# A graph layer's product held back for the last scatter, a table tile read in five parts, and its loads moved to another queue

## The chip, the cores and the metric

The kernel runs on one core of a Trainium2 chip. The core has five engines that this text names as the profile does: PE (TensorE, matrix products; PEld is its weight load), DVE (VectorE), ACT (ScalarE), POOL (GpSimd) and SP (SyncE, which here only issues transfers). [...] The metric is device microseconds of one launch, median of several runs.

## The reference

The input is a matrix x of 625 nodes by 1024 features and a list of 10,000 edges. Two layers follow each other. What matters here is layer 0:

```python
xn = layernorm(x)
x = x + gnn(xn, edges) + mix(xn)            # a graph attention, and a linear attention with an output product W_o
x = x + ffn(layernorm(x))                   # a product with weights rounded to -1, 0, 1
# gnn: for each edge e: s -> d and each of 4 heads
score[e, h] = sum_k leaky_relu(xl[s, h, k] + xr[d, h, k]) * att[h, k]
out[d, h]   = sum_e softmax_over_edges_into_d(score)[e, h] * xl[s, h]
# gnn ends with out @ W_up
```

Layer 1 has another graph step, another linear attention, and a feed-forward part with eight experts of which each node uses two; it takes the larger part of the time.

## The kernel before, in words

The 625 nodes are five tiles of 125 rows (`NT` = 5, `P` = 125). Nearly all products are in float32, with a moving side of 512 or 313 columns. In layer 0 the graph attention and the linear attention are computed side by side.

**Edge scores.** POOL gathers the rows xl and xr of each edge (`gather`, L621), 128 edges at a time and two such chunks to a group; DVE turns them into scores (`score_group`), ACT takes the exponential (L608), and POOL scatters the four numbers of each edge into a table in DRAM with a row per pair of nodes (`scatter`, L641). All scatters write one DRAM tensor, so each waits for the landing of the one before. Every node's edge to itself is written by ACT's queue (`self_loops`). CT, in SBUF, counts how often each pair of nodes occurs.

**Pacing.** The order of the instructions on each engine is written by hand. `do(prep, pe, after)` records a step: PE's part now, and its `after` part when the next step is recorded. `work(us)` adds to a planned time, and as it grows `one_beat` records one more group's gathers, scores and scatters between the products of the linear attention. What is left of the beats is recorded in the loop `while chunks: one_beat()`.

**Around the change.** `mixed(t)` (L758) is the output product of the linear attention for node tile t, in two halves c of 512 columns, each of 8 matmuls (`cs` selects halves); it leaves its sum open in PSUM, for `up_again` to add the graph attention to. The end of the edge stage records mixed(3), the rest of mixed(0), then mixed(1) and mixed(2) with `ternary`, the rounding of the feed-forward weights on DVE (L801, L802, L804) between them, and then the remaining beats. mixed(4) comes later, as the PSUM of tile 0 comes free.

After the last scatter, for each node tile p in turn:
- `load_table(p)` reads tile p of the table, `tb`, 125 partitions by five rows of 2000 bytes (500 numbers) each, 1.25 MB, through `rows_dma`, which splits every load into 112 and 13 partitions;
- `weigh(p)` multiplies it with CT on DVE, one instruction for each of the five source tiles s (L865), giving pT;
- `sums(p)` has 20 small matmuls of PE (pg: 4 heads by 5 source tiles), whose result DVE divides (dens, den, go; L898 to L902);
- `turn_sums(p)` transposes it, and `up_again(p)` adds its product with W_up to px and then, on DVE, px to x (L933);
- `ffn(p)` is the feed-forward part of tile p, in steps put between the others.

The rows of x are loaded again for this (L1056), and `add_bias` (L1072) adds the output bias to them. In the kernel before POOL issues all of this: table tile 0, x tile 0, table tile 1, then x tiles 1 to 4, and table tiles 2 to 4 as buffers of the pool `mid` come free. SP issues the weights (`Half`, L124), among them the key and value weights of layer 1 (`lin1.weights`).

[...]

Of the kernel before, what the change touches and what calls it, by code (L numbers as in the profile page):

```python
# [14 lines left out]
ALU = mybir.AluOpType  # L15
# [5 lines left out]
NT = 5  # L21
P = 125
# [31 lines left out]
def attempt(ctx: ExitStack, tc: tile.TileContext, w: dict, out: bass.AP, shifted: bool):  # L54

    nc = tc.nc
# [83 lines left out]
    latest = {}  # L140

    def behind(ins, name):

        tc.add_manual_dep(ins.ins, name, mybir.DependencyInfo(mybir.DependencyClass.Sync,
                                                              mybir.DependencyReason.DATA), reason="pace")
        return ins
# [31 lines left out]
    def rows_dma(eng, dst, src):  # L178

        return [eng.dma_start(out=dst[lo:hi], in_=src[lo:hi]) for lo, hi in ((0, 112), (112, P))]  # L180
# [6 lines left out]
    xrows = w["x"].rearrange("(t p) d -> t p d", p=P)  # L187
# [34 lines left out]
    do = Stream()  # L222
    hold = {}
# [139 lines left out]
    with ExitStack() as st0:  # L363
# [5 lines left out]
        tview = table[0:N * N, :].rearrange("(u p d) h -> p u (d h)", u=NT, p=P)  # L369
        xnT = bigT("xnT")  # L370

        with ExitStack() as edges:
# [263 lines left out]
            def scatter(last):  # L636

                if chunks and chunks[0][0] <= min(last, beat["raised"] - 1):
                    g, j = chunks.pop(0)
                    lo, n, p = groups[g]  # L640
                    nc.gpsimd.indirect_dma_start(  # L641
                        out=table[:, :],
                        out_offset=bass.IndirectOffsetOnAxis(ap=at[0:p, lo + j:lo + j + 1], axis=0),
                        in_=es[0:p, lo + j, :], in_offset=None)

            own = pool.tile([P, NT, 4], FP, name="own")
            linear = pool.tile([P, NT, 4], FP, name="linear")
# [40 lines left out]
            def raise_all(last):  # L688
                while beat["raised"] <= min(last, beat["scored"] - 1):
                    lo, n, p = groups[beat["raised"]]  # L690
                    exp(es[0:p, lo:lo + n, :])
                    beat["raised"] += 1

            def one_beat():
                g = beat["g"]
                beat["g"] += 1
                if 5 <= g < NT + 5:
                    self_loops(g - 5)
                if lags[1] > lags[0]:
                    raise_all(g - lags[1])  # L700
                    scores(g - lags[0])
                else:
                    scores(g - lags[0])
                    raise_all(g - lags[1])
                for j in range(G):
                    if g < len(groups):
                        gather(g, j, 0)
                        scatter(g - lags[2] - 1)
                        gather(g, j, 1)
                    scatter(g - lags[2])  # L710
# [47 lines left out]
            def mixed(t, ks=range(KC), keep=None, then=None, paced=True, cs=(0, 1)):  # L758
                for c in cs:
                    def pe(c=c):  # L760
                        if c == 0 and ks[0] == 0:
                            hold["px", t] = ps2("px1")
                        for k in ks:
                            made = nc.tensor.matmul(hold["px", t][:P, c, :], lhsT=oT[:, k, nodes(t)], rhs=wo[c](k),  # L764
                                                    start=(k == 0), stop=(k == KC - 1 and keep is not None))
                        latest["pe"] = made.ins.name

                    def after():
                        px = hold.pop(("px", t))
                        for c in range(2):  # L770
                            nc.vector.tensor_tensor(keep[:, c, :], px[:P, c, :], bo[c][:P], op=ALU.add)

                    do(None, pe, after if keep is not None and c == 1 else None)
                    if then is not None and c == 0:
                        then()
                    if paced:
                        work(0.87 * len(ks))
# [21 lines left out]
            def ternary(i):  # L799
                v = raw[i]  # L800
                nc.vector.tensor_scalar(v, v, wscale[:, i:i + 1], 1.0, op0=ALU.mult, op1=ALU.min)  # L801
                nc.vector.tensor_scalar(v, v, -1.0, MAGIC, op0=ALU.max, op1=ALU.add)  # L802
                m = made[i]
                nc.vector.tensor_scalar(m, v.rearrange("p (k n) -> p k n", k=m.shape[1]), MAGIC, None,  # L804
                                        op0=ALU.subtract)
# [21 lines left out]
            bo = [lin.bias(w["L0_bo"], c, tag) for c, tag in enumerate(("bk_t", "bv_t"))]  # L827
            dn = mix.tile([128, 2, D], BF, tag="kv", name="dn", bufs=2)
            gu = wpool.tile([128, KC, 512], BF, tag="w", name="gu", padded_shape=[128, KC, 512])
            made = [gu[:, :, 0:256], gu[:, :, 256:512], dn]  # L830
            lags[:] = 1, 1, 2
            kept = mid([P, 2, 512], "kept")
            mixed(3, keep=kept, then=weight_sums)
            mixed(0, range(6, KC))
            weight_means()
            for t in (1, 2):
                mixed(t)
                ternary(t)
            ternary(0)
            do.flush()  # L840
            while chunks:
                one_beat()
            if not shifted:
                test_linear()

        xpool = ctx.enter_context(tc.tile_pool(name="xpool", bufs=1, side="right", reuse_waits="tile"))
        x = xpool.tile([P, NT, D], FP, name="x")
# [3 lines left out]
        def load_table(t):  # L851

            hold["tb", t] = mid([P, NT, P, 4], "tb")
            if not shifted:
                rows_dma(nc.gpsimd, hold["tb", t].rearrange("p s d h -> p s (d h)"),
                         tview[:, :, t * 4 * P:(t + 1) * 4 * P])

        def weigh(t):

            tb, pT = hold.pop(("tb", t)), mid([P, NT, 4, P], "pT")  # L860
            hold["pT", t] = pT
            if shifted:
                exps(t, tb)
            for s in range(NT):
                nc.vector.tensor_tensor(pT[:, s], tb[:, s].rearrange("p d h -> p h d"),  # L865
                                        CT[:, s, nodes(t)].unsqueeze(1).to_broadcast([P, 4, P]), op=ALU.mult)
# [184 lines left out]
            return p1, f1, f2, f3, f4, p5, f5  # L1051


        load_table(0)
        for t in range(NT):
            rows_dma(nc.gpsimd, x[:, t, :], xrows[t])  # L1056
            if t == 0:
                load_table(1)
        weigh(0)
        kv_pieces = iter([(f, t) for t in range(NT) for f in ("key", "value")])  # L1060
        made_of = {}

        def spacer():

            f, t = next(kv_pieces)
            getattr(lin1, f)(t)

        def add_bias(*ts):
            for t in ts:
                for c in range(2):  # L1070
                    xc = x[:, t, c * 512:(c + 1) * 512]
                    nc.vector.tensor_tensor(xc, xc, kept[:, c, :] if t == 3 else bo[c][:P], op=ALU.add)  # L1072

        degree = mix.tile([128, NP], mybir.dt.int16, tag="degree", name="degree", bufs=1)

# [8 lines left out]
        for p in range(NT + 2):  # L1084
            do()
            if p >= 2 and p != NT:
                made_of[p - 2][5]()
            if 1 <= p <= NT:
                made_of[p - 1] = ffn(p - 1)
                made_of[p - 1][0]()  # L1090
            if p == 1:
                mixed(4, cs=(0,))
            if p == 2:
                add_bias(2, 4)
                in_degrees()
            if p >= 3:
                spacer()
            if p >= 2 and p != NT:
                made_of[p - 2][6]()
            if p == 0:  # L1100
                xnT1 = bigT("xnT1")
                nc.gpsimd.memset(xnT1[:, :, N:NP], 0.0)
                lin1 = LinearAttention(xnT1, ("L1_Wq", "L1_Wk", "L1_bk", "L1_Wv", "L1_bv"), w["L1_bq"],
                                       lambda us: None, nc.gpsimd)
                lin1.large = True
            if p < NT:
                sums(p)
            if 1 <= p <= NT:
                made_of[p - 1][1]()
                do()  # L1110
                if p == NT:
                    made_of[p - 2][5]()
                made_of[p - 1][2]()
                if p == NT:
                    made_of[p - 2][6]()
            do()
            if p < NT:
                turn_sums(p)
            if p + 1 < NT:
                weigh(p + 1)  # L1120
            if p + 2 < NT:
                load_table(p + 2)
            if p < 2:
                add_bias(*((0, 1), (3,))[p])
            if p == 1:
                mixed(4, cs=(1,))
                lin1.weights(0)
                lin1.half(0, loaded=True)
            if 2 <= p <= NT:
                spacer()  # L1130
            if 1 <= p <= NT:
                made_of[p - 1][3]()
            do()
            if p < NT:
                up_again(p)
            if 1 <= p <= NT:
                made_of[p - 1][4]()
# [568 lines left out]
    for i in range(2):  # L1706
# [5 lines left out]
        first = small(f"first{i}")  # L1712
# [41 lines left out]
    for i in range(3):  # L1754
        d = 1 << i
# [240 lines left out]
```

## Time and profile before

| | us |
|---|---|
| median of 3 runs | 2182.63 (2180.21 to 2184.75) |
| the profiled execution | 2200.8 |
| its span, from the first to the last instruction | 2199.0 |
| PE busy | 2106.0 (96%) |
| DVE busy | 713.1 (32%) |
| POOL busy | 340.3 (15%) |
| ACT busy | 194.7 (9%) |
| longest wait of PE, before the first pg matmul | 31.4 |

The profile page gives busy time by engine, and groups of instructions by source line. Its timeline gives, for each run of equal instructions, the start and length in us, the engine, the line, the operation, output and input tile and shape, the count, and in brackets how long the engine had been idle before and what ended that. [...] A float32 matmul shows as two records of PE: the 8 matmuls of half a mixed product are 16. The mean rate of the transfers over the span is 137 GB/s.

### The profile page before, as it was taken

To read this page: it belongs to the slowest core of one execution; us is meant where nothing else is said; L and a number is where in the kernel's file an instruction comes from. 1 tells how busy PE (TensorE), PEld (TensorE's weight loads), DVE (VectorE), ACT (ScalarE), POOL (GpSimd) and SP (SyncE) were. 2 spreads that over 40 slices of the span, in tenths; PEclk is the share of its full clock that TensorE was granted. 3 is DMA by queue.
4 is the path that set the end of the run, shared out by engine and by line. 5 is a ranking of instruction groups with operands and counts; after the bars stand their busy time and mean duration, and the time that the engine had idled before them with its cause. 6 is when DMAs were issued, how large, how long until landed. Compare 5 with 4: busy or idle time off the path is not lost. (4 is left out here: it accounts for less than half of the span.)

```text
span 2199.0 us, 17371 instructions
## 1 busy us (share of the span) xinstructions
PE 2106.0 (96%) x6934; PEld 1205.2 (55%) x6934; DVE 713.1 (32%) x1214; ACT 194.7 (9%) x355; POOL 340.3 (15%) x349
## 2 busy tenths in 40 slices
PE   7989999489899999999999999999999999999998
PEld 6656575155445777754446777457744444444443
DVE  5776478367532740000122143222111111111012
ACT  2000110012211100000000111100000000000000
POOL 1666756500000200210000000110000000000011
PEclk9999999789999999999999999999999999999999
DMA  7623253261122110150203101022099988997742
GB/s 216 205 77 106 81 182 123 58 174 33 39 86 77 48 39 26 62 182 0 101 14 106 59 18 39 29 95 96 28 365 343 330 291 308 331 329 283 277 140 91
DMA packets 145848, 301.62 MB, mean 137 GB/s; under 512 B 12370, under 2 KB 22436, under 8 KB 145754
## 3 DMA queue, kind: packets, MB, share of 16 engines
q1 hardware_dynamic: 123700, 244.23, 31.3%
q0 software_dynamic: 17376, 46.42, 7.3%
q10 hardware_dynamic: 4678, 9.72, 1.4%
q8 instruction: 58, 0.95, 0.2%
q14 instruction: 36, 0.29, 0.0%
HBM read 277.49 MB, written 22.84 MB: 137 GB/s over the span
## 5 line engine op out<-in xcount | busy, mean ns | idle before, releaser
L137 PE MATMUL pu<-w,xgT 128*128 128x512 f32 x768 | 333.9, 593 | 1.9 <-DVE xgT L1290 1.9
L137 PEld LDWEIGHTS pu<-w,xgT 128*128 128x128 f32 x768 | 144.0, 190 | 174.8 <-issue 172.0
L137 PE MATMUL pyb<-w,hb 128*128 128x512 f32 x384 | 174.3, 598 | 2.5 <-ACT yb L105 2.1
L137 PE MATMUL pk<-w,xnT 128*125 128x512 f32 x320 | 144.7, 606 | 2.3 <-ACT xnT L1047 2.2
L137 PE MATMUL pv<-w,xnT 128*125 128x512 f32 x320 | 143.4, 599 | 1.8 <-DVE x L933 0.9
L137 PE MATMUL pq<-xnT,w 128*128 128x313 f32 x512 | 139.1, 430 | 0.9 <-DVE v L293 0.8
L137 PE MATMUL p<-tT,w 128*128 128x313 f32 x512 | 136.3, 428 | 0.4 <-DVE tT L1290 0.4
L137 PEld LDWEIGHTS pq<-xnT,w 128*128 128x128 f32 x512 | 97.7, 192 | 40.3 <-DVE v L293 1.6
L137 PEld LDWEIGHTS pyb<-w,hb 128*128 128x128 f32 x384 | 69.8, 189 | 90.9 <-issue 74.8
L1830 DVE TENSOR_TENSOR su<-pu,su 128x512 f32<-128x512 f32 x24 | 16.6, 691 | 314.6 <-ACT su L1829 314.6
L137 PEld LDWEIGHTS p<-tT,w 128*128 128x128 f32 x512 | 96.8, 190 | 37.9 <-issue 1.2
L137 PEld LDWEIGHTS pk<-w,xnT 128*125 128x125 f32 x320 | 60.8, 193 | 76.7 <-issue 74.0
L137 PEld LDWEIGHTS pv<-w,xnT 128*125 128x125 f32 x320 | 60.2, 190 | 76.5 <-issue 74.2
L641 POOL DMA_INDIRECT table<-es,at x79 | 84.0, 1063 | 56.4 <-issue 27.7
L1813 POOL DMA_INDIRECT xg<-rows_d,slots x12 | 11.4, 950 | 524.7 <-PE pxg L1820 448.9
L621 POOL DMA_INDIRECT ga<-xl_d,si x79 | 80.1, 1013 | 52.4 <-issue 20.1
L621 POOL DMA_INDIRECT gb<-xr_d,di x79 | 80.5, 1019 | 25.3 <-issue 24.7
L764 PE MATMUL px<-w,oT 128*125 128x512 f32 x160 | 69.8, 594 | 2.2 <-DVE x L933 1.6
L1179 DVE TENSOR_TENSOR z<-pz,z 125x512 fp32r<-125x512 f32 x10 | 6.9, 692 | 196.8 <-ACT z L1177 196.8
L137 PE MATMUL px<-w,hT 128*125 128x512 f32 x160 | 70.3, 592 | 0.0
L137 PE MATMUL px<-w,oT 128*125 128x512 f32 x160 | 70.3, 592 | 0.0
L137 PE MATMUL ph<-meanT,w 128*128 128x313 f32 x256 | 70.0, 426 | 0.0
(364 smaller groups left out, 2509.6 us busy)
## 6 DMA issues: line engine op xcount, KB each, us to landing
w<-in_eW_dram SPq DMA_DIRECT2D x144, 1024.0 KB
w<-in_L_Wk_dram SPq DMA_DIRECT2D x8, 1024.0 KB
w<-in_L_Wv_dram SPq DMA_DIRECT2D x8, 1024.0 KB
w<-in_L_Wq_dram SPq DMA_DIRECT2D x8, 1024.0 KB
w<-in_L_Wo_dram SPq DMA_DIRECT2D x8, 1024.0 KB
w<-in_W_self_dram SPq DMA_DIRECT2D x8, 1024.0 KB
w<-in_W_neigh_dram SPq DMA_DIRECT2D x8, 1024.0 KB
w<-in_sW_dram SPq DMA_DIRECT2D x8, 1024.0 KB
```

Of the source, the lines that this page charges most:

```text
L137: made = nc.tensor.matmul(dst, lhsT=lhsT, rhs=rhs, start=(i == 0), stop=(i == len(pairs) - 1))
L621: got = nc.gpsimd.indirect_dma_start(out=ab[g][side][0:p, j, :], out_offset=None, in_=src[:, :], in_offset=bass.IndirectOffsetOnAxis(ap=ix ...
L641: nc.gpsimd.indirect_dma_start(out=table[:, :], out_offset=bass.IndirectOffsetOnAxis(ap=at[0:p, lo + j:lo + j + 1], axis=0), in_=es[0:p, l ...
L764: made = nc.tensor.matmul(hold["px", t][:P, c, :], lhsT=oT[:, k, nodes(t)], rhs=wo[c](k), start=(k == 0), stop=(k == KC - 1 and keep is no ...
L1179: nc.vector.tensor_tensor(low, src, high.bitcast(FP), op=ALU.subtract)
L1813: nc.gpsimd.indirect_dma_start(out=xg, out_offset=None, in_=rows_d[:, :], in_offset=bass.IndirectOffsetOnAxis(ap=slots[:, b:b + 1], axis=0))
L1830: nc.vector.tensor_tensor(su, pu[:, 0, :], su, op=ALU.mult)
```

## The change

1. The second half of mixed(2) is taken out of its place and recorded after the last beat. Its first matmul gets an added wait for the landing of the last scatter. The first half stays, and ternary(2) and ternary(0) follow it; with less planned work recorded, the last group of edges is scored in a later beat, behind all three conversions on DVE. The orders of POOL up to the last scatter are the same.
2. Table tile 0 is read in five loads, one for each source tile, in turn by SP and ACT; each of the five instructions of weigh(0) waits for its own part. The other table tiles are read by SP in one load, as they were by POOL.
3. The rows of x are loaded by SP: x tiles 0 and 1, then table tile 1, then x tiles 2 to 4.
4. The bias is added to x tiles 0 and 1 just after weigh(0), ahead of the divisions of tile 0; before, this stood after weigh(1).

```diff
@@ -638,10 +638,11 @@
-                    nc.gpsimd.indirect_dma_start(
+                    put = nc.gpsimd.indirect_dma_start(
                         out=table[:, :],
                         out_offset=bass.IndirectOffsetOnAxis(ap=at[0:p, lo + j:lo + j + 1], axis=0),
                         in_=es[0:p, lo + j, :], in_offset=None)
+                    latest["scatter"] = put.ins.name
@@ -763,6 +764,8 @@
                             made = nc.tensor.matmul(hold["px", t][:P, c, :], lhsT=oT[:, k, nodes(t)], rhs=wo[c](k),
                                                     start=(k == 0), stop=(k == KC - 1 and keep is not None))
+                            if k == 0:
+                                latest["first"] = made
                         latest["pe"] = made.ins.name
@@ -833,13 +836,17 @@
             weight_means()
-            for t in (1, 2):
-                mixed(t)
-                ternary(t)
+            mixed(1)
+            ternary(1)
+            mixed(2, cs=(0,))
+            ternary(2)
             ternary(0)
             do.flush()
             while chunks:
                 one_beat()
+            mixed(2, cs=(1,), paced=False)
+            behind(latest["first"], latest["scatter"])
+            do.flush()
             if not shifted:
                 test_linear()
@@ -851,8 +858,12 @@
             hold["tb", t] = mid([P, NT, P, 4], "tb")
-            if not shifted:
-                rows_dma(nc.gpsimd, hold["tb", t].rearrange("p s d h -> p s (d h)"),
+            if not shifted and t == 0:
+                for s in range(NT):
+                    rows_dma((nc.sync, nc.scalar)[s % 2], hold["tb", t][:, s].rearrange("p d h -> p (d h)"),
+                             tview[:, s, t * 4 * P:(t + 1) * 4 * P])
+            elif not shifted:
+                rows_dma(nc.sync, hold["tb", t].rearrange("p s d h -> p s (d h)"),
                          tview[:, :, t * 4 * P:(t + 1) * 4 * P])
@@ -1051,25 +1062,26 @@
-        load_table(0)
-        for t in range(NT):
-            rows_dma(nc.gpsimd, x[:, t, :], xrows[t])
-            if t == 0:
-                load_table(1)
-        weigh(0)
...
+        load_table(0)
+        for t in range(NT):
+            rows_dma(nc.sync, x[:, t, :], xrows[t])
+            if t == 1:
+                load_table(1)
+        weigh(0)
+        add_bias(0, 1)
@@ -1120,8 +1132,8 @@
             if p + 2 < NT:
                 load_table(p + 2)
-            if p < 2:
-                add_bias(*((0, 1), (3,))[p])
+            if p == 1:
+                add_bias(3)
```

`add_bias` itself is moved up in the source, unchanged.

## The prediction

> **What bounds the kernel now.** I read the page first. Its slices show TensorE (PE) at 7 to 9 tenths everywhere except slice 7 (385 to 440 us), which shows 4. The waits view, PE alone, then gives one wait of size, 31.4 us, of the first sum (pg) on the weighting of the edge table (pT, L865). The next longest is 9.6 us, at the start. So the end is set by PE, and what the change can win lies in or just behind this hole. The timeline of 370 to 480 us, GpSimd (POOL) alone, shows what fills the hole (start, length, engine, line, tile, idle before it and its releaser):
>
> ```profile
> 423.64 0.96 POOL L641 DMA_INDIRECT table<-es,at  x1 [1.40 <-DMA table<-es,at]
> 426.50 0.85 POOL L641 DMA_INDIRECT table<-es,at  x1 [1.91 <-issue]
> 429.02 1.55 POOL L180 DMA_DIRECT2D tb<-table  x2 [1.67 <-issue]
> 430.55 1.11 POOL L180 DMA_DIRECT2D x<-in_x_dram  x2
> 431.64 1.46 POOL L180 DMA_DIRECT2D tb<-table  x2
> ...
> 444.86 0.55 POOL L180 DMA_DIRECT2D x<-in_x_dram  x1 [4.33 <-DMA tb<-table]
> 445.94 0.52 POOL L180 DMA_DIRECT2D x<-in_x_dram  x1 [0.54 <-DMA tb<-table]
> ```
>
> Each scatter waits for the landing of the one before. The last has landed by 429.0, when the first table tile is asked for. The two waits at 444.86 and 445.94 are for the landings of the second tile. On VectorE (DVE) and PE, the same view:
>
> ```profile
> 437.42 4.83 DVE L865 TENSOR_TENSOR pT<-tb,CT 125x500 f32<-125x500 f32 x5 [16.36 <-DMA tb<-table]
> 450.07 4.87 DVE L865 TENSOR_TENSOR pT<-tb,CT 125x500 f32<-125x500 f32 x5
> 457.25 1.24 DVE L933 TENSOR_TENSOR x<-px,x 125x1024 f32<-125x1024 f32 x1
> 438.51 0.68 PE L137 MATMUL pg<-xl,pT 125*125 125x65 f32 x2 [31.40 <-DVE pT L865]
> 442.30 6.98 PE L137 MATMUL pg<-xl,pT 125*125 125x65 f32 x32 [0.26 <-DVE pT L865]
> 451.42 5.52 PE L928 MATMUL px<-wu,goT 128*125 128x512 f32 x8 [0.53 <-ACT goT L916]
> 458.54 7.13 PE L764 MATMUL px<-w,oT 128*125 128x512 f32 x16 [1.59 <-DVE x L933]
> 465.50 4.48 PE L137 MATMUL pg<-xl,pT 125*125 125x65 f32 x40
> 480.61 3.60 PE L928 MATMUL px<-wu,goT 128*125 128x512 f32 x8
> ```
>
> Weighting starts only when the whole tile is there (437.42). Sum 0 ends at 449.3. The next dense product, mixed(4), starts at 458.54, once L933 frees its PSUM tile. From there PE runs nearly without holes, and later weights wait for PE (the waits of SP: 319.5 us on pu, 180.0 on pq). So **the start of mixed(4) carries the whole rest of the kernel**, and I forecast that one time. The pg rows take 0.218 us each here and 0.112 in sum 1. The stretches view says why (PE, PEld, DVE, ACT, POOL busy; then granted clock, DMA share, GB/s):
>
> ```profile
> 449.00:451.00 2.00, 0.96 (x4) 0.38 (x3) 1.61 (x4) 0.01 (x1) 1.41 (x2) 0.50 0.97 232
> 455.00:456.00 1.00, 1.00 (x4) 0.52 (x3) 1.00 (x2) 0.00 (x0) 0.00 (x0) 0.94 1.05 254
> ```
>
> PE is at half clock from the hole until about 455.07, 3.65 us into the first dense product. The sums themselves did not raise it.
>
> [...]
>
> **The change, part by part, in the profiled execution.**
>
> 1. *Scatters.* POOL's order and waits up to the last scatter are the same in both programs. On DVE the last score group (1.5 us) now stands behind all three conversions (3.8 us each), so the last exponential moves from 413.2 to about 420.8. The last scatter needs it at 426.5: 5.7 us of cover, past which each us would count. The conversions run in one piece, so scatters may stretch differently, by up to 0.8 us either way. Landing stays at 429.0.
>
> 2. *The held half product.* 8 matmuls leave 16 records of 0.433 us (27.71/64, L764): 7.0 us at full clock. They leave PE before the hole, which only starts earlier (400.2 for 407.1), since POOL sets its end. In the hole they start at 429.0 at half clock: 3.65 us give 4.2 records, the other 11.8 take 5.1, end 437.8. [...] I take 437.8. Queued behind it on PE is sum 0, nothing else.
>
> 3. *First tile in five parts, SP and ACT.* First bytes came 1.6 us after asking on POOL (45 GB/s over 429 to 431). On SP they came 1.6 us after the Wk request at 462.26 and about 1.1 us after the first one of the kernel. So 430.4. The five parts are 1.25 MB. POOL moved such tiles at 200 to 250 GB/s; SP at the kernel's start, 2.9 MB from 2 to 13 us, 265. I take 260. Parts 0 and 1 share the engines: 0.5 MB, 1.9 us, plus about 1.2[...] (the old tile's bytes were through at about 435.4 and it counted as landed at 436.9 to 437.4, 1.5 to 2.0 for a whole tile): 433.5. [...] part 4 is asked for only when part 1 has landed: a bubble of 0.8 us; it lands at about 437. Weighting at 1.05 a part: 433.5 to 438.8, for 442.25.
>
> 4. *Sum 0 at full clock.* Three quarters of it follow the last part: 15 matmuls, 30 records of 0.112, 3.4 us after 438.8; or 4.5 us after the half product at 437.8. End 442.3, for 449.3. Then dens, den, go: 443.2. ACT's four tile requests stand ahead of goT, but are gone by 434.
>
> 5. *x and second tile on SP.* Order: x0, x1, second tile. 1.25 + 1.0 + 1.25 = 3.5 MB at 260 are 13.5 us; 430.4 + 13.5 + 0.8 + 1.2 = **445.9**. Before, x0 alone stood ahead of it and it landed at 445.94. This is what is late next: weighting 1 could start at 443.2 and waits 2.7 us. Bounds: 300 GB/s gives 444.1, 210 gives 449.1.
>
> 6. *Bias of tiles 0 and 1.* Four adds of about 0.6 us (454.84 to 457.25) go ahead of sum 0's divisions. x1 is there 1.25 MB (4.8 us) before the second tile, at 441.1; its two adds end at 442.3, under sum 0. So L933 follows weighting 1 at once: 2.4 us off the path.
>
> 7. *Sum.* 445.9 + 4.9 (weighting 1) + 1.24 (L933) + 0.1 = 452.1, for 458.54: **6.4 us less**. PE's product with wu is done by about 448.2 (443.2 + 1.4 for turning + 3.6), so it does not set this.
>
> 8. *SP's queue.* The table tiles now stand ahead of L1's weights. Tile 3 waits for sum 1 (470.0, then 463.6), so Wk is asked for at about 464.5 instead of 462.26, behind a 5 us tile: landed by about 477, Wv by 483. The first key product comes at 502.96, then 496.5. Cover 19 us for Wk; without it every us late is a us of PE. POOL loses ten pairs of requests; what stays on it waits for DVE anyway (26.6 us at bk_t).
>
> The profiled execution took 2200.8 us (span 2199.0); minus 6.4 is 2194.4. The runs' median is 2182.63, 0.8% less; I carry the difference over unscaled: **2176.2 us**.
>
> **Rivals.**
> - *Loads no limit.* If SP's loads reach 300 GB/s or more (weights at 464 to 466 ran at 362), the second tile is there by 444.1 or before go is done (443.2), and mixed(4) starts at 449.4 to 450.3: 8.2 to 9.1 us less, about 2174. Against: [...] tile 3, alone, moved at 252.
> - *Loads no faster than on POOL, or PE cold again.* At 210 GB/s mixed(4) starts at 455.3, 3.2 us less; 2179.4. PE then idles from 448.2 for 7 us, may fall to half clock, and mixed(4) pays up to half of 3.65 us: 1.4 us less in all. Even the main case leaves 3.9 us idle[...]; after its start this trace has no other PE wait of 3 us or more to price it, so 0 to 1.8. I take 0 for the likeliest[...].
> - *Slower[...].* [...] If latency and not rate rules, x0, x1 and the second tile crawl. The deciding point is the second tile landing at 452.3, that is 3.5 MB at 176 GB/s; at 145 it lands at 456.5, 4.2 us late, and with the cold clock (1.8) the kernel takes 2188.6. For it: single 2 us stretches at 137 and 176 GB/s. [...]
> - *The half product does not warm PE.* It ends at 442.9 and sum 0 (8.7 us at half clock) at 451.6, so nothing is won; the rise at 455.07 speaks against it. It goes with the slower case.
>
> **How the numbers follow.** 0.2% is 4.4 us, about what a measurement of this kernel can tell from no change. Main case, 5 to 7.5 us less: 0.48. Loads no limit: 0.22. Loads slow or cold, 0 to 4.4 less: 0.22. The rest, slower: 0.08. So faster 0.70, same 0.22, slower 0.08. The main case's own range is 2175 to 2178. With the fast case and most of the slow one, and a us for the medians: 2172.5 to 2182.
>
> **What would show it.** Half clock ending inside the half product, which ends near 438; pg rows at 0.112 from the first; weighting 0 starting near 433.5 with gaps of about a us at most; weighting 1 waiting for the second tile, not for PE; mixed(4) at 452; Wk landed long before its product. The forecast is wrong if SP moves this mix far from 260 GB/s, if the last scatter shifts by more than a us, or if PE is at half clock in mixed(4).

## The result, and the profile after

The changed kernel takes 2175.97 us (median of 9 runs, 2173.66 to 2179.04), the kernel before 2179.61 us on the same occasion (9 runs, 2177.78 to 2184.75). The ratio is 0.998, 95% interval 0.9971 to 0.9989: 2.4 to 6.3 us less, on the edge of what a measurement can tell from no change. The forecast was 2176.2 us, 6.4 less than the 2182.63 shown first. The time was met; the gain was a little over half of the forecast one, and the base had moved.

Executions differ by 20 us and more before the last scatter lands (at 428.4 us in the profile of before, at 405.9 in that of after). This goes with the chip and not with the change: the changed kernel, run again on another chip, had it at 429.1, and in the profiles of the experiments it was at 424.6 to 438.1 us on two chips and at 407.2 to 407.8 on two others. So whole profiled times can't be set against each other. In what follows t0 is 1.94 us after the last scatter's request starts on POOL, when PE's held product is let go in the changed kernel, and times are counted from it. (A request's row on POOL is shorter than its transfer: this one's is 0.85 us long in the changed kernel, and PE's wait for the landing ends 1.94 us after its start.) The prediction took 429.0, POOL's next request, for it. A product is called warm when the stretches view shows a granted clock of 1.00 under it and cold when it shows 0.50 (half clock: 0.218 us for a record of sum 0 in the profile of before, 0.112 at full clock); the held half is the second half of mixed(2). Two more products of PE come up below: pdn, the second product of a node tile's feed-forward part (here tile 0's), and pdeg, which counts the edges into each node from CT (the in-degree product).

The timeline of the changed kernel, PE and DVE (start, length, engine, line, operation, tiles, count, idle before it and its releaser), to be read against the same lines of before:

```profile
405.94 9.60 PE L765 MATMUL px<-w,oT 128*125 128x512 f32 x16 [28.43 <-DMA table<-es,at]
409.99 4.93 DVE L876 TENSOR_TENSOR pT<-tb,CT 125x500 f32<-125x500 f32 x5 [12.03 <-DMA tb<-table]
415.37 4.48 PE L137 MATMUL pg<-xl,pT 125*125 125x65 f32 x40
421.74 5.09 PE L939 MATMUL px<-wu,goT 128*125 128x512 f32 x8 [0.53 <-ACT goT L927]
423.20 4.89 DVE L876 TENSOR_TENSOR pT<-tb,CT 125x500 f32<-125x500 f32 x5 [2.48 <-DMA tb<-table]
427.99 1.23 DVE L944 TENSOR_TENSOR x<-px,x 125x1024 f32<-125x1024 f32 x1
429.28 7.13 PE L765 MATMUL px<-w,oT 128*125 128x512 f32 x16 [2.45 <-DVE x L944]
...
456.26 1.02 PE L137 MATMUL pdn<-dn,room 128*125 128x512 bf16 x4 [1.31 <-DVE x L944]
...
458.79 7.17 PE L137 MATMUL pdeg<-CT,ones 125*128 125x313 f32 x20 [1.50 <-DVE x L1042]
```

The rows show the order that was forecast: the held half at once at t0, weighting 0 beginning 4.05 us after t0 (before: 9.0), sum 0 in 4.48 us without a gap, then weighting 1 waiting 2.48 us for the second tile, and mixed(4) (L765, second time) at t0 + 23.34, for t0 + 30.10 before: 6.76 us earlier. But from there to the end of the span are 1742.52 us, for 1740.46 before: 2.06 us are given back. Two rows show half clock. The product with wu (8 records in 5.09 us, a warm one takes 3.6) had it before, too (5.52 us). New is pdeg: 7.17 us, for 5.54 in the kernel before, whose waits around pdn are the same:

```profile
485.52 1.02 PE L137 MATMUL pdn<-dn,room 128*125 128x512 bf16 x4 [1.32 <-DVE x L933]
488.05 5.54 PE L137 MATMUL pdeg<-CT,ones 125*128 125x313 f32 x20 [1.50 <-DVE x L1031]
```

The stretches view of the changed kernel has the granted clock in the third number from the end:

```profile
418.00:420.00 2.00, 1.85 (x17) 1.71 (x16) 1.08 (x3) 0.00 (x0) 0.00 (x0) 1.00 1.05 265
422.00:424.00 2.00, 2.00 (x3) 0.90 (x4) 0.80 (x1) 0.98 (x1) 0.00 (x0) 0.50 1.05 254
...
458.00:460.00 2.00, 1.21 (x3) 0.84 (x4) 1.97 (x5) 0.00 (x0) 0.00 (x0) 0.68 0.27 98
460.00:462.00 2.00, 2.00 (x5) 1.34 (x4) 1.60 (x5) 0.29 (x1) 0.00 (x0) 0.50 0.00 0
```

### The profile page after: what moved, and what is told of

Same layout as the page of the kernel before. It is cut to its first block, busy times and chain, and to the rows that moved or that the text cites. A ratio compares the mean times of both kernels' runs of the same rounds, so it can differ in the third digit from the quotient of the medians.

```text
span 2171.8 us, 17390 instructions
## 1 busy us (share of the span) xinstructions
PE 2094.0 (96%) x6934; PEld 1198.0 (55%) x6934; DVE 711.9 (33%) x1214; ACT 194.8 (9%) x355; POOL 328.4 (15%) x329
## 5 line engine op out<-in xcount | busy, mean ns | idle before, releaser
L765 PE MATMUL px<-w,oT 128*125 128x512 f32 x160 | 72.5, 611 | 30.9 <-DMA table<-es,at 28.4
```

## The experiments

Three questions: which of the four parts brings the earlier start of mixed(4); whether that start really carries the rest; where the clock takes its share. Ratios are against the kernel before on the same chip, with 95% intervals; the chips differ (before had medians of 2204.30, 2207.57, 2180.39 and 2179.51 us in the four groups).

| kernel | mixed(4) starts, t0 + | it takes | pdeg takes | its start to the end | t0 to the end | ratio |
|---|---|---|---|---|---|---|
| before | 30.10 | 7.13 | 5.54 | 1740.46 | 1770.56 | 1 |
| changed | 23.34 | 7.13 | 7.17 | 1742.52 | 1765.86 | 0.9980 (0.9971 to 0.9989) |
| changed, again | 24.83 | 9.81 | 7.22 | 1745.21 | 1770.04 | 0.9988 (0.9976 to 1.0000) |
| no held half | 26.34 | 7.13 | 5.54 | 1740.78 | 1767.12 | 0.9977 (0.9961 to 0.9994) |
| tile 0 in one load | 29.08 | 7.13 | 5.54 | 1740.94 | 1770.02 | 0.9993 (0.9975 to 1.0012) |
| loads on POOL | 35.81 | 7.13 | 5.54 | 1741.28 | 1777.09 | 1.0026 (1.0016 to 1.0035) |
| bias late | 26.08 | 8.80 | 6.97 | 1743.74 | 1769.82 | 0.9993 (0.9973 to 1.0012) |
| before + held half | 30.09 | 7.13 | 5.54 | 1740.66 | 1770.75 | 0.9995 (0.9976 to 1.0014) |
| before + 12 held | 27.24 | 8.83 | 7.23 | 1743.58 | 1770.82 | 1.0000 (0.9979 to 1.0020) |
| degrees in the hole | 24.35 | 8.83 | - | 1745.70 | 1770.05 | 1.0005 (0.9992 to 1.0019) |
| wait filled | 24.70 | 7.13 | 5.54 | 1740.51 | 1765.21 | 0.9978 (0.9970 to 0.9986) |
| tile 1 in parts | 20.14 | 7.13 | 5.54 | 1740.67 | 1760.81 | 0.9975 (0.9958 to 0.9993) |
| tile 1 in parts, again | 23.03 | 7.13 | 5.54 | 1740.89 | 1763.92 | 0.9964 (0.9949 to 0.9979) |
| and degrees split | 20.28 | 7.13 | 2 x 2.80 | 1746.48 | 1766.76 | 0.9993 (0.9985 to 1.0001) |

The first columns are from one profiled execution of each, the ratio from all of its runs. Two profiles of one kernel differ by 1.5 us (changed) and 2.9 us (tile 1 in parts) at mixed(4), so single differences of that size prove nothing.

**One part left out at a time.** First the held half: mixed(2) whole in its old place.

```diff
+            for t in (1, 2):
+                mixed(t)
+                ternary(t)
-            mixed(1)
-            ternary(1)
-            mixed(2, cs=(0,))
-            ternary(2)
...
-            mixed(2, cs=(1,), paced=False)
-            behind(latest["first"], latest["scatter"])
-            do.flush()
```

> The changed kernel with the whole of mixed(2) back in its old place, nothing held. t0 is the landing of the last scatter; in the changed kernel mixed(4) starts at t0 + 23.34. Theory L (the landing of the second tile at t0 + 17.3 sets what follows, the held half is mostly absorbed by it): weighting 0 as in the changed kernel (t0 + 4 to 9), sum 0 at half clock (0.218 us a record, 30 records after the last part) ends at about t0 + 15.6, go at t0 + 16.5, still ahead of the second tile; the product with wu runs t0 + 17.9 to 23.4 at half clock and sets the rest: mixed(4) at t0 + 24.7, 1.4 us later than in the changed kernel, and as much later in the whole. Theory H (the held half is the main gain): mixed(4) 3 us or more later, at t0 + 26.5 or beyond.

The timeline, the sum and the second weighting:

```profile
439.94 6.98 PE L137 MATMUL pg<-xl,pT 125*125 125x65 f32 x32 [0.26 <-DVE pT L872]
449.19 4.86 DVE L872 TENSOR_TENSOR pT<-tb,CT 125x500 f32<-125x500 f32 x5 [1.40 <-DMA tb<-table]
```

Sum 0 is at half clock (0.218 us a record) and yet done before the second tile is there: weighting 1 still waits 1.40 us for it. The product with wu, cold for 6.45 us, then sets the start of mixed(4), as theory L says. mixed(4) starts 3.0 us later than in the changed kernel's first profile and 1.5 later than in its second, but none of what follows is at half clock. From t0 to the end it stands between the two (1767.12; 1765.86 and 1770.04), and its ratio is no worse. So, by these three profiles, the held half wins 1.5 to 3.0 us at mixed(4) and 1.7 to 4.4 are lost again behind it. No run here shows that it is worth anything in the whole.

Then the first tile in one load on SP.

```diff
-            if not shifted and t == 0:
-                for s in range(NT):
-                    rows_dma((nc.sync, nc.scalar)[s % 2], hold["tb", t][:, s].rearrange("p d h -> p (d h)"),
-                             tview[:, s, t * 4 * P:(t + 1) * 4 * P])
-            elif not shifted:
+            if not shifted:
                 rows_dma(nc.sync, hold["tb", t].rearrange("p s d h -> p s (d h)"),
```

> The changed kernel with the first tile read by one load on SP, no parts. Theory L: the tile lands at about t0 + 7.8 (1.25 MB at 240 GB/s, and 2.6 us around it), weighting 0 runs to t0 + 12.7, sum 0 ends at about t0 + 16.1, go at t0 + 17.0, just ahead of the second tile at t0 + 17.3; mixed(4) at t0 + 24.8 if the product with wu is at half clock, 23.5 if not: 0 to 1.4 us later than the changed kernel. Rival (the parts are what brings the gain): everything after weighting 0 is later by the 3.7 us that it is later, mixed(4) at t0 + 27.

Its timeline:

```profile
429.78 10.02 PE L765 MATMUL px<-w,oT 128*125 128x512 f32 x16 [29.42 <-DMA table<-es,at]
437.60 4.88 DVE L872 TENSOR_TENSOR pT<-tb,CT 125x500 f32<-125x500 f32 x5 [15.79 <-DMA tb<-table]
...
442.54 6.98 PE L137 MATMUL pg<-xl,pT 125*125 125x65 f32 x32 [0.51 <-DVE pT L872]
```

The tile landed at t0 + 7.8, as expected, but mixed(4) came at t0 + 29.1, worse than both theories. The reason is in the third row: the bulk of sum 0 is at half clock, although the held half had ended at 439.8 at full clock and the first sums followed it at once. From 440.2 to 442.5 PE only had the sums of single parts, 0.43 us in each 0.95, and the clock fell at 442.44. In these profiles the held half left sum 0 warm where the weighting ended with it or soon after: 0.8 us later (changed, again) and 1.4 us later (12 held, below) were soon enough, 2.7 us (here) was not. The parts are what brings that about.

The bias of tiles 0 and 1 behind weighting 1, as before:

```diff
-        add_bias(0, 1)
...
-            if p == 1:
-                add_bias(3)
+            if p < 2:
+                add_bias(*((0, 1), (3,))[p])
```

> The changed kernel with the bias of tiles 0 and 1 added after weighting 1, as before the change. Theory L: weighting 1 still ends at t0 + 22.2, and the four adds (2.76 us) stand between it and the sum that frees the PSUM tile: mixed(4) at t0 + 26.1, 2.8 us later, which is most of the difference between the two kernels; the whole 2.8 us later. Rival (what the start of mixed(4) wins is given back further on, since the rest of the kernel has slack or changes its clock): mixed(4) 2.8 us later, the whole less than 1 us later.

```profile
456.76 8.80 PE L765 MATMUL px<-w,oT 128*125 128x512 f32 x16 [4.75 <-DVE x L944]
```

mixed(4) starts 2.74 us later than in the changed kernel, as the four adds predict (2.76), and then costs 1.67 more, since PE idled 4.75 us ahead of it and the clock fell at 456.73, to rise again at 460.14. From t0 to the end it stands 4.0 us above the changed kernel's first profile and 0.2 below its second, so the whole doesn't tell the two theories apart.

x and the later tiles on POOL:

```diff
-                rows_dma(nc.sync, hold["tb", t].rearrange("p s d h -> p s (d h)"),
+                rows_dma(nc.gpsimd, hold["tb", t].rearrange("p s d h -> p s (d h)"),
...
-            rows_dma(nc.sync, x[:, t, :], xrows[t])
+            rows_dma(nc.gpsimd, x[:, t, :], xrows[t])
```

> The changed kernel with x and the tables' tiles 1 to 4 asked for by POOL again (x0, x1, second tile, x2 ...), the first tile in five parts on SP and ACT as in the change. Theory L (the 16 engines are the limit, the queue does not matter): x and the second tile now share the engines with the parts from the start, weighting 0 runs to t0 + 10 to 12 with gaps, the second tile lands at t0 + 17 to 19. If the weighting still ends by about t0 + 10, sum 0 is at full clock and mixed(4) starts at t0 + 23.3 to 25, as in the changed kernel; if it ends later, with gaps between the parts, the clock drops and mixed(4) is at t0 + 26 or later. Rival (SP moves these loads faster than POOL): second tile 2 us or more later than t0 + 17.3 to 18.8, with the weighting as in the changed kernel.

Weighting 0 in its timeline:

```profile
415.96 2.01 DVE L876 TENSOR_TENSOR pT<-tb,CT 125x500 f32<-125x500 f32 x2 [16.12 <-DMA tb<-table]
...
420.60 1.98 DVE L876 TENSOR_TENSOR pT<-tb,CT 125x500 f32<-125x500 f32 x2 [2.62 <-DMA tb<-table]
...
426.26 1.03 DVE L876 TENSOR_TENSOR pT<-tb,CT 125x500 f32<-125x500 f32 x1 [3.68 <-DMA tb<-table]
...
427.35 6.98 PE L137 MATMUL pg<-xl,pT 125*125 125x65 f32 x32 [4.03 <-DVE pT L876]
```

This is the one experiment clearly slower than before. POOL asks for x from 406.73, before the scatter has landed (407.81), since x doesn't depend on it; from 406 to 427 its queue moved 3.45 of 4.70 MB. The last of the five parts landed at t0 + 18.5; in the changed kernel it was there by t0 + 8. The 16 DMA engines were as busy as in the changed kernel (93% of 406 to 427 at 224 GB/s; there 89% of 404 to 432 at 222 GB/s): SP's loads were not faster, but with x behind the parts on SP the parts went first. Here x was also asked for 1.1 us before t0, ahead of the parts; no run separates that from its having a queue of its own. What the trace shows is that the loads on POOL's queue were not kept back for the parts: with SP's three parts (0.75 MB) and ACT's two (0.50 MB) under way, POOL's 3.45 MB moved in the same 21 us.

**One part alone.** The held half added to the kernel before, then a longer one.

```diff
...
+            mixed(2, cs=(1,), paced=False)
+            behind(latest["first"], latest["scatter"])
+            do.flush()
```

> The kernel before with the held half product alone; loads all on POOL, one load a tile, bias late. Theory L: half product t0 to 9.4, weighting 0 as before (t0 + 8.4 to 13.3), sum 0 at full clock ends at about t0 + 16.7 for 20.3, go at t0 + 17.5, the second tile being there since t0 + 16.9: weighting 1 to t0 + 22.4, bias to t0 + 25.2, mixed(4) at t0 + 26.5, for t0 + 29.5 before: 3.0 us less in the whole. The half product thus wins more alone than it costs to take it out of the changed kernel. If its effect were the same alone as in the changed kernel, it would be 1.4 us. If it does not raise the clock, 0.

```profile
424.56 8.61 PE L765 MATMUL px<-w,oT 128*125 128x512 f32 x16 [28.43 <-DMA table<-es,at]
...
438.42 6.98 PE L137 MATMUL pg<-xl,pT 125*125 125x65 f32 x32 [0.52 <-DVE pT L872]
```

Nothing is won, neither at mixed(4) nor in the whole. The product ends at 433.2, the weighting at 438.4; from 434.6 on PE has the sums of single parts, 0.43 us in each 0.95, and the clock is down at 437.81, 0.6 us before the bulk of the sum. With 12 matmuls held for 8:

```diff
...
+            mixed(2, range(4, KC), cs=(0,), paced=False)
+            behind(latest["first"], latest["scatter"])
+            mixed(2, cs=(1,), paced=False)
+            do.flush()
```

> The kernel before with a longer held product alone: 12 matmuls (24 records) of mixed(2) for 8, all else as before (loads on POOL, one load a tile, bias late). With 8 held, the product ended 4.4 us ahead of the weighting's end, the sums came one by one behind the parts (0.43 us in each 0.95) and the clock was down again when the bulk of sum 0 ran: mixed(4) at t0 + 30.1, as before. Theory G (what counts is that the held work reaches to the sum without a gap): 24 records end at about t0 + 12.3 to 13, the bulk of sum 0 runs at 0.112 us a record and ends at t0 + 16.7, mixed(4) at t0 + 26.5 to 27: 3 us less in the whole. Rival (the sums' own light work drops the clock whatever stands ahead): sum 0 at 0.218, no gain.

```profile
438.09 12.74 PE L765 MATMUL px<-w,oT 128*125 128x512 f32 x24 [36.15 <-DMA table<-es,at]
452.32 3.71 PE L137 MATMUL pg<-xl,pT 125*125 125x65 f32 x32 [0.52 <-DVE pT L873]
465.32 8.83 PE L765 MATMUL px<-w,oT 128*125 128x512 f32 x16 [3.70 <-DVE x L941]
```

The sum is at full clock (3.71 us for 32 records) and mixed(4) starts 2.86 us earlier than before. That speaks against the rival: the sums were cold with PE busy 0.43 us in each 0.95 ahead of them (before + held half), not by themselves. And still nothing is won in the whole. PE is 5.0 us earlier at the end of the product with wu, but 2.1 of these turn into a longer wait ahead of mixed(4) (3.70 us for 1.59, since DVE with weighting 1 and bias is the longer branch), and the rest is lost at half clock: mixed(4) takes 1.70 us more and pdeg 1.69.

**Where the gain is given back.** The changed kernel again:

> The changed kernel itself once more, beside the experiments. Counted from t0 (1.94 us after the last scatter's request starts on POOL), mixed(4) starts at t0 + 23.3 for t0 + 30.1 in the kernel before: 6.8 us earlier. Theory C ([...]pdeg at half clock in the changed kernel's profile was chance): pdeg takes 5.5 us, the whole is 6 to 7 us less, ratio 0.997. Theory S (the shift puts pdeg systematically on a clock drop): pdeg 7.2 us again, the whole is 5 us less, ratio 0.9977.

```profile
447.85 4.85 DVE L876 TENSOR_TENSOR pT<-tb,CT 125x500 f32<-125x500 f32 x5 [4.40 <-DMA tb<-table]
453.89 9.81 PE L765 MATMUL px<-w,oT 128*125 128x512 f32 x16 [4.02 <-DVE x L944]
...
486.07 7.22 PE L137 MATMUL pdeg<-CT,ones 125*128 125x313 f32 x20 [1.50 <-DVE x L1042]
```

Here the second tile landed 1.5 us later (t0 + 18.8), PE waited 4.02 us, and mixed(4) took 2.68 us more and pdeg 1.68: of 5.27 us won at mixed(4), 4.75 were given back. The first nine runs of the kernel fit such a spread: four at 2173.7 to 2173.9 us, all with a mean granted clock of 0.988, and five at 2176.0 to 2179.0, the two longest with 0.986. Only two executions are traced, and the first of them is the fastest of its nine. To test the wait ahead of mixed(4) as the cause, part of mixed(2) is moved from ahead of the hole into this wait; PE's work is the same.

```diff
-            mixed(2, cs=(0,))
+            mixed(2, range(5), cs=(0,))
...
+                mixed(2, range(5, KC), cs=(0,), paced=False)
                 mixed(4, cs=(0,))
```

> The changed kernel with three matmuls (6 records, 2.6 us at full clock) of mixed(2)'s first half taken from ahead of the hole and put between the product with wu and mixed(4), where PE waits 2.45 to 4.0 us for the second tile's weighting. PE does the same work, 2.6 us of it later. Theory G (what the change wins at the start of mixed(4) is given back because a wait of over 2.4 us there, and the one behind pdn, lets PE fall to half clock): mixed(4) starts at t0 + 23.4 to 24.8 and always takes 7.1 us (9.8 in the changed kernel's second profile), from there to the end some 1740.5 to 1742.5 us for 1745.2, and the whole is 1.5 to 3 us less than the changed kernel's. Rival (the loss lies elsewhere): no change, or the 1 us by which the 2.6 us overfill the shortest wait.

```profile
428.40 2.74 PE L765 MATMUL px<-w,oT 128*125 128x512 f32 x6
...
432.19 7.13 PE L765 MATMUL px<-w,oT 128*125 128x512 f32 x16 [1.06 <-DVE x L944]
...
461.70 5.54 PE L137 MATMUL pdeg<-CT,ones 125*128 125x313 f32 x20 [1.50 <-DVE x L1042]
```

The second tile was late here too (t0 + 18.6), but mixed(4) and pdeg are at full clock, and from mixed(4) to the end it takes 1740.51 us, as before. Of all profiles with a wait of at most 2.45 us ahead of mixed(4) none has it slow; all four with 3.27 us or more have. That shows the cause at mixed(4); for pdeg see the last section. In the whole the 1.5 to 3 us that were expected don't show: its ratio, 0.9978, can't be told from the changed kernel's.

**Versions that might beat both.** The second tile in parts too:

```diff
-            if not shifted and t == 0:
+            if not shifted and t < 2:
                 for s in range(NT):
-                    rows_dma((nc.sync, nc.scalar)[s % 2], hold["tb", t][:, s].rearrange("p d h -> p (d h)"),
+                    rows_dma(nc.scalar if t == 0 and s % 2 else nc.sync,
+                             hold["tb", t][:, s].rearrange("p d h -> p (d h)"),
```

> The changed kernel with the second tile, too, read in five parts (all on SP). If the landing of the whole second tile (t0 + 17.3) is what is late next: weighting 1 starts when go is done (t0 + 14.8) and ends 1 us after the last part, at about t0 + 18.6 to 19.6 for 22.2; then the product with wu (ends t0 + 20.9, part of it at half clock) sets the sum that frees the PSUM tile: mixed(4) at t0 + 22.2, 1.1 us earlier. If the request of ten pieces on one queue holds them up, no gain or up to 1 us later.

```profile
445.71 4.89 DVE L877 TENSOR_TENSOR pT<-tb,CT 125x500 f32<-125x500 f32 x5
446.81 3.70 PE L940 MATMUL px<-wu,goT 128*125 128x512 f32 x8 [0.53 <-ACT goT L928]
451.83 7.13 PE L765 MATMUL px<-w,oT 128*125 128x512 f32 x16 [1.32 <-DVE x L945]
```

Weighting 1 starts behind go without a wait and without gaps, so the second tile was indeed what was late next. The product with wu is warm this time, mixed(4) starts at t0 + 20.1, and PE's wait is 1.32 us, with mixed(4) warm. Once more:

> The kernel with the second tile, too, in five parts, once more, to price it as a version of its own. In its first profile mixed(4) started at t0 + 20.1 and all behind it took 1740.7 us, as in the kernel before. If mixed(4)'s start is the whole effect, the kernel takes 9.5 to 10 us less than before, ratio 0.9955. If the clock takes part of it back in most executions, 4 to 7 us less, ratio 0.997 to 0.998.

Here the product with wu was cold (5.37 us) and mixed(4) started at t0 + 23.0, with 1740.89 behind it. The median is 2172.41 us for 2179.51 (8 and 13 runs), ratio 0.9964. Its two ratios are the lowest measured here; their intervals overlap the changed kernel's. The first ratio hides a wide spread: of its 22 runs, 10 took 2190.5 to 2199.2 us and 12 took 2204.3 to 2217.3, so that its median, 2204.46, is no lower than the changed kernel's on the same chip (2203.69), and the profile is of one of the 10. The time goes with the clock: among the 8 runs made again, from 2168.4 us at a mean granted clock of 0.991 to 2178.8 at 0.985. That this version beats the changed kernel is not shown.

The in-degree product, 5.5 us of PE that need no table, moved into the hole:

```diff
+            for h in range(2):
+                def pe(h=h):
+                    hold["pdeg", h] = ps1("pdeg")
+                    group(hold["pdeg", h][:, :HN], [(ones[:P, :], CT[:, s, h * HN:(h + 1) * HN]) for s in range(NT)])
...
                 add_bias(2, 4)
-                in_degrees()
```

> The changed kernel with the in-degree product (pdeg, 20 records) taken from behind tile 0's pdn and put into the hole ahead of the held half, where PE waits for scatters anyway. mixed(4) at t0 + 23.3 as in the changed kernel. Behind pdn PE then waits for the normalised tile (VectorE, ready some 4.5 us after pdn) instead of running pdeg for 5.5 to 7.2 us. If the clock stays up: sum 2 starts 2.7 to 4.0 us earlier and the whole is 2.5 to 4 us less than the changed kernel. If the 4.5 us without work drop the clock: sum 2 takes 9 us for 4.5 and nothing is won (0, or up to 1 us later).

```profile
492.75 1.93 PE L1064 MATMUL ptr<-ident,xn 125*128 125x125 f32 x8 [4.05 <-DVE xn L1056]
495.45 8.66 PE L137 MATMUL pg<-xl,pT 125*125 125x65 f32 x40 [0.77 <-ACT xnT L1065]
```

The 5.5 us of work had covered DVE's work on the tile. Without it PE waits 4.05 us and runs sum 2 at half clock (8.66 us for 4.48): nothing won, as the second half of the expectation has it. Splitting it around pdn, on top of the second tile in parts:

```diff
...
+            if p == 1:
+                in_degrees(0)
             if 1 <= p <= NT:
                 made_of[p - 1][4]()
+            if p == 1:
+                in_degrees(1)
```

> The kernel with the second tile in five parts as well (mixed(4) started at t0 + 20.1), and the in-degree product split in two halves in single banks, one ahead of pdn and one behind it, which fills the waits of 1.3 and 1.5 us around pdn. mixed(4) again at about t0 + 20.1 if the product with wu is warm, t0 + 22 if not. Behind tile 1's product with wu: half 0 (2.8 us), pdn, half 1 (2.8 us), then PE waits 1.5 to 2 us for the normalised tile; sum 2 starts about 1.1 us earlier than with pdeg in one piece, and pdeg is never at half clock. The whole is 1 us less than with the second tile in parts alone, 9 to 11 us less than before, ratio 0.995 to 0.996. If VectorE, now later by the 1.5 us that pdn is later, sets the rest, 0.

```profile
462.33 1.90 PE L1058 MATMUL ptr<-ident,xn 125*128 125x125 f32 x8 [3.00 <-DVE xn L1050]
464.94 8.66 PE L137 MATMUL pg<-xl,pT 125*125 125x65 f32 x40 [0.71 <-ACT xnT L1059]
```

It filled the two small waits (pdeg 2 x 2.80, warm) and made a single one of 3.00 us behind them, during which the clock fell (at 461.61), and sum 2 was cold: from mixed(4) to the end 5.8 us more than with the second tile in parts alone.

## Why the prediction was right or wrong

1. *Scatters.* Right as to the cover: the last exponential was at 397.5, the last scatter's request at 404.0. Three scatters stand beside the conversions in both profiles, with 1.52 to 2.31 us each on POOL before and 1.81 to 2.17 now (the three behind them have 0.85 to 0.96 in both): 0.25 us more in sum, within the 0.8 allowed. Whether the landing moved by a us can't be told; on one chip it varied from 424.6 to 430.7 us between profiles.
2. *The held half product.* Right in mechanism and size: 8.6 to 10.1 us in the profiles that hold 16 records, for 8.8. The clock rose 2.9 to 6.1 us after t0, for 3.65, each time on the grid of the last section. (In the trace of before it rose at 455.13, 3.71 us into the product; 455.07 and 3.65 are slightly misread.)
3. *First tile in parts.* Right: weighting 0 at t0 + 4.05 to 4.46 for t0 + 4.5, without gaps. The bubble of 0.8 us does not show in it: SP's request for part 4 starts at 409.67, 2.12 us behind the end of its request before, and the five instructions still run through in 4.93 us.
4. *Sum 0.* Right: warm, ending at t0 + 13.9 and 13.2 for 13.3 (32 records, not 30, follow the last part in the kernel before). What the step didn't say is that the held half wins this only with the parts: alone it wins nothing.
5. *Second tile.* Landed at t0 + 17.3 and 18.8 for 16.9, and was late next, as said.
6. *Bias.* Right: 2.74 us for 2.4.
7. *Sum.* mixed(4) at t0 + 23.3 and 24.8 for 23.1: right. **What failed is what the first part put in bold, that its start carries the whole rest, and the price of the cold clock, "0 to 1.8. I take 0".** Behind it 2.06 and 4.75 us were given back. A sign that the prediction itself named, PE at half clock in mixed(4), showed in the second profile. The wait ahead of mixed(4) was foreseen (3.9 us; it was 2.45 and 4.02), but its price of 0 was the author's estimate, with no trace behind it. Not foreseen were that the clock fell after stretches with work in them, too (1.34 us of 3.41, below), that the loss reached 2.7, and that pdeg lost another 1.7 behind waits of 1.3 and 1.5 us with 1.0 us of work between. With those the net is 4.7 and 0.5 us in the two profiles; it is 4.4 and 2.6 us by the two ratios, 3.6 and 3.9 by the medians. The loss at mixed(4) comes from the change, which makes the wait longer. For pdeg this isn't shown: the kernel before has the same two waits, and one profile doesn't say how often its own pdeg is cold. This is the rival "PE cold again", given 0.22 together with slow loads, added to the main case rather than in its place.
8. *SP's queue.* Right: the first key product waited for no weights. The slower case did not come: the second tile landed 4.5 us or more ahead of that rival's deciding point (t0 + 23.3); that latency and not rate would rule there was the author's estimate. What the step missed is what the move to SP is for: with the loads left on POOL the kernel takes 5.6 us more than before by the medians (2185.94 for 2180.39), since x then shares the engines with the parts, the last of which lands at t0 + 18.5.

The product with wu was forecast warm and was cold in both profiles of the changed kernel (5.09 and 5.39 us), hidden because weighting 1 ended later. That the time itself came out within 0.3 us is luck: the median of before, 2182.63 us in three runs, was 2179.61 in nine, so 3 us of the 6.4 were in the base, about as much as the gain fell short.

## What to carry to other kernels

Here a stage that got faster on PE but still waited for another engine turned its gain into idle time, and waits of 3.27 us and more were paid for at half clock a little later (1.7 to 2.7 us in mixed(4)). Where a trace shows the like, shorten the branch that the wait ends on, or fill the wait with held work, before speeding up PE; here both kept mixed(4) warm, though the runs don't settle what they are worth in the whole. Work that looks misplaced may be the cover that keeps PE busy (pdeg: without its 5.5 us PE waited 4.05 us, and sum 2 took 8.66 us for 4.48). And a load that others wait for was protected here by standing first in a queue that it shares (the first tile was there by t0 + 8), not by a queue of its own (t0 + 18.5 with x on POOL).

## What the runs showed of the hardware that was not expected

- The clock's changes lie on one grid. In the changed kernel they are at 410.93 (up), 421.17 (down), 424.58 (up), 458.72 (down) and 462.13 (up): 10.24, 3.41, 34.14 and 3.41 us apart, 3, 1, 10 and 1 times 3.41. Over the whole spans of before and of the changed kernel all changes (14 and 12) lie on such a grid within 0.01 us, and so do those between 380 and 500 us in each of the other twelve profiles. Against t0 the grid falls differently in each profile. A step below is the 3.41 us from one point of it to the next.
- The clock fell after steps in which PE was not idle. Steps with 0.80 and 1.56 us of PE's work in 3.41 (changed, again: ahead of mixed(4), and around pdn), 1.02 (changed, around pdn), 1.34 (degrees in the hole, ahead of mixed(4)) and 1.62 us (before + 12 held, around pdn) were followed by half clock; steps with 1.58 (no hold, around pdn), 1.79 (wait filled, around pdn), 1.91 (tile 1 in parts, around pdn) and 2.13 us (changed, ahead of mixed(4)) were not. So between 1.56 and 1.62 us, a little under half of the step, both happened, and the time alone gives no sharp line. Two pairs of neighbouring steps, changed and no hold:

```profile
455.30:458.72 3.42, 1.02 (x4) 0.41 (x3) 2.43 (x5) 0.00 (x0) 0.00 (x0) 1.00 0.94 347
458.72:462.13 3.41, 3.34 (x7) 2.23 (x8) 2.98 (x8) 0.29 (x1) 0.00 (x0) 0.50 0.04 16
...
481.94:485.35 3.41, 1.58 (x6) 0.54 (x4) 2.20 (x5) 0.00 (x0) 0.00 (x0) 1.00 1.05 388
485.35:488.77 3.42, 2.43 (x9) 1.81 (x10) 2.99 (x8) 0.29 (x1) 0.00 (x0) 1.00 0.16 58
```

- Under the sums of 65 columns the recorded busy time did not tell the clock. In the kernel before, a step of them with PE recorded as busy for all 3.41 us at half clock (444.89 to 448.30) was not followed by full clock, while one of the dense product with wu, busy as long (451.72 to 455.13), was. At full clock a step with 3.39 us of sums was followed by full clock (changed, again); one with 2.5 us of PE's records, 2.1 of them sums, by half clock (changed, 421.17). The steps of before and of changed, again, each with the next:

```profile
444.89:448.30 3.41, 3.41 (x18) 3.41 (x18) 0.00 (x0) 0.00 (x0) 1.76 (x4) 0.50 1.03 252
448.30:451.72 3.42, 1.97 (x8) 1.39 (x8) 2.33 (x5) 0.72 (x2) 1.46 (x2) 0.50 1.01 242
...
438.83:442.24 3.41, 3.39 (x32) 3.25 (x30) 2.07 (x4) 0.00 (x0) 0.00 (x0) 1.00 0.99 252
442.24:445.65 3.41, 1.61 (x5) 0.87 (x6) 1.15 (x4) 1.59 (x2) 0.00 (x0) 1.00 1.07 211
```

- Whether pdeg was cold went with how the waits around pdn (1.3 and 1.5 us) fell on this grid. It was cold in four of the twelve profiles that run it in one piece behind pdn, each with sum 0 warm; three others with sum 0 warm have it at full clock. In the four, pdn began 0.3 to 1.4 us after the start of a step, in the other eight, before among them, 1.9 to 3.1 us. How often either kernel meets it is left open.
